# Seven products for the first q and k of an attention kernel, too, and more of V's fold beside the first scores

## The chip, the core and the metric

The kernel runs on one core of a Trainium2 chip, in one launch. The metric is the device time of an execution in microseconds (us). A core has TensorE (matrix products, with weight loads beside them), VectorE, ScalarE, GpSimd and SyncE, which here only issues DMAs. In profiles they are PE (with PEld), DVE, ACT, POOL and SP; L403 is line 403 of the kernel. Each engine works through its own instructions in order and waits for others by semaphores.

## What is computed

Four batches of 1024 tokens of width 512 go through attention, an LSTM-like gate with a causal convolution, and a feed-forward product, each followed by a layer norm. Only the attention is touched. Each of q, k, v comes from two linear layers one after the other:

```python
q = _lin(_lin(x, wq_w, wq_b), vq_w, vq_b)      # likewise k and v
q = q.reshape(b, s, hc, H).transpose(2, 0, 1, 3)   # 32 heads of 16
scores = jnp.einsum('cbqh,cbkh->cbqk', q, k) / scale
attn = jax.nn.softmax(scores, axis=-1)
o = jnp.einsum('cbqk,cbkh->cbqh', attn, v)
```

All is float32.

## The kernel before

**Folds.** The two layers of each of q, k, v are multiplied into one 512x512 matrix ("fold"), w_q, w_k (L384) and w_v (`fold_v`, L546: eight pieces of 16 matmuls, four row tiles times four column quarters, 256 columns each). The bias of the second layer plus the image of the first layer's bias is made on VectorE by `bias()` (L362 to L369). V's bias, a column, is turned into a row through DRAM: L800 writes b_d from b_vc, one element per descriptor, and L801 loads it into all partitions as b_v.

**Units, pairs and quadrants.** 32 units (batch, group of four heads). Two units make a pair p: 128 columns of w. q and k of a pair are made packed, 16 rows per head; `to_quadrants(u, which, packed)` (L398) then copies the four heads of a unit to partitions 0, 32, 64, 96 by four DMAs of 64 KB from SyncE's queue (L403). There are four such slots for q and four for k (u % 4).

**Two ways to q and k.** `project` (L407), in `qk_pieces` (L419) cut into six pieces of 176 or 160 columns, multiplies the pair's 128 columns of w by x directly: 16 matmuls per piece, with the bias added by ScalarE as it copies the result out of PSUM (L414). Only pairs 0 and 1 (units 0 to 3) are made this way. All later pairs come by twos from a scheme of Strassen's kind with seven products instead of eight (`product`, L482; `products`, L518): the 512x256 block of w and x are cut into 2x2 blocks, GpSimd makes the four sums of w's blocks (`sum_w`, L456, through `sum_blocks`, L459) and of x's (`sums_of_x`, L439; the last of the four writes over a block of x), TensorE does seven products of 8 matmuls for each 256 columns, ScalarE copies each out of PSUM (L498, L500), and GpSimd adds them together (L503 to L514). Products 2, 3 and 4 go to one of four `rooms` of 256 columns first. c11 and c12 of the result are the first pair, c21 and c22 the second.

**V.** V is made in the same way with seven products (`v_products`, L556). Of batch 0, products 1 to 3 are added by VectorE straight from PSUM (L579 to L583, with b_v, and L588); products 4 to 7 are copied to two rooms by ScalarE (L572) and added by GpSimd (L585, L588).

**Order.** It is written out by hand; in this part nothing is scheduled by a tool. A head comes first: warm-up matmuls, the folds of q and k, two pieces of `early` into PSUM tiles of `early_ps`, the rest of pair 0's q, its k, five of V's eight folds (`folds[:5]`, L794). GpSimd does the first three sums of x (L444 to L446) and pair 2's sums for q (L463 to L466) meanwhile. Then a first stage (u = -1, L851) makes only the row maxima of unit 0's scores, 32 pieces `nat` of two matmuls each (L616), whose maxima VectorE takes (L632, and L628 for those in single PSUM tiles). It goes in eleven steps, each of up to three score pieces followed by a share of `fill`: the rest of the folds, pair 1's q and k (12 pieces), the sums of V and x, 14 pieces of V, and the first six pieces of pairs 2 and 3. All pieces, and every second score piece (`apart`, two of them), take turns in the four PSUM tiles `st`; the other score pieces have two tiles of their own. After that each stage u does the exponentials of unit u and the maxima of u + 1, again with fill between.

The calls around the change:

```python
    for piece in early[2:] + qk_pieces(0, 1) + folds[:5]:        # L794
        piece()
    late_sum = sums_of_x(0)
    for work in late_sum[:3]:
        work()
    sum_w(2, 0)
    nc.sync.dma_start(b_d.rearrange("(t p) -> p t", p=P), b_vc)  # L800
    nc.sync.dma_start(b_v, b_d.partition_broadcast(P))           # L801
```

Of the kernel before, what the change touches and what calls it, by code (L numbers as in the profile page):

```python
# [8 lines left out]
F32 = mybir.dt.float32  # L9
AF = mybir.ActivationFunctionType  # L10
ALU = mybir.AluOpType
# [3 lines left out]
P = 128  # L15
B, S, D = 4, 1024, 512
# [36 lines left out]
def by_quarters(nc, pt, lhsT, rhs, tiles=FT):  # L53


    for f in range(tiles):
        for j in range(4):
            r = slice(32 * j, 32 * j + 32)
            nc.tensor.matmul(pt[r, :], lhsT(f)[:, r], rhs(f), start=f == 0, stop=f == tiles - 1)  # L59
# [193 lines left out]
def attention(ctx, tc, a, attn_d, ident, shared, hand):  # L253
# [7 lines left out]
    b_k = const.tile([P, FT], F32, tag="b_k", name="b_k")  # L261
    b_v = shared.tile([P, D], F32, tag="b_f", name="b_v")

    def big_slot(b, name):
        return shared.tile([P, NT * (D + 1)], F32, tag=f"big{b % 2}", name=name)

# [81 lines left out]
    for which, (w, v, dst) in enumerate((("wq", "vq", b_q), ("wk", "vk", b_k), ("wv", "vv", None))):  # L348
        w_n = sp.tile([P, FT, D], F32, tag="w_n", name=f"w_n{which}")
        v_t = sp.tile([P, FT, D], F32, tag="v_t", name=f"v_t{which}")  # L350
        for m in range(FT):
            rows = slice(m * P, (m + 1) * P)
            nc.sync.dma_start(w_n[:, m, :], a[f"{w}_w"][rows, :])

            (nc.scalar if which == 0 else nc.sync).dma_start(v_t[:, m, :], a[f"{v}_wT"][rows, :])
        v_n = w_v if which == 2 else rows_of_v[:, which * FT : (which + 1) * FT, :]
        w_b = sp.tile([P, D], F32, tag="w_b", name=f"w_b{which}")
        v_b = sp.tile([P, FT], F32, tag="v_bc", name=f"v_b{which}")
        if dst is None:
            dst = sp.tile([P, FT], F32, tag="b_vc", bufs=1, name="b_vc")  # L360

        def bias(w=w, v=v, dst=dst, v_n=v_n, w_b=w_b, v_b=v_b):  # L362

            nc.sync.dma_start(v_n, a[f"{v}_w"].rearrange("(t p) m -> p t m", p=P))
            nc.sync.dma_start(w_b, a[f"{w}_b"].partition_broadcast(P))
            nc.sync.dma_start(v_b, a[f"{v}_bc"])
            nc.vector.tensor_mul(v_n, v_n, w_b.unsqueeze(1).to_broadcast([P, FT, D]))
            nc.vector.tensor_reduce(dst, v_n, AX.X, ALU.add)
            nc.vector.tensor_add(dst, dst, v_b)  # L369

        if which == 2:
            bias()
            b_d = dpool.tile([D], F32, tag="b_v", bufs=1, name="b_vd")
            b_vc = dst
            break
        if which == 1:
            xts[0] = load_x(0)
        bias()
        w_d = (w_q, w_k)[which]

        pts = [ps.tile([P, D], F32, tag="ps", name=f"fold{which}_{f}") for f in range(FT)]
        for m in range(FT):
            for f in range(FT):
                nc.tensor.matmul(  # L384
                    pts[f], w_n[:, m, f * P : (f + 1) * P], v_t[:, m, :], start=m == 0, stop=m == FT - 1
                )
        for f in range(FT):
            if f % 2:
                nc.scalar.copy(w_d[:, f, :], pts[f])
            else:  # L390
                nc.vector.tensor_copy(w_d[:, f, :], pts[f])
# [6 lines left out]
    def to_quadrants(u, which, packed):  # L398
# [4 lines left out]
            nc.sync.dma_start(dst[32 * j : 32 * j + HD, :], packed[h * HD : (h + 1) * HD, :])  # L403
        if which == 0 and u >= 4:
            nc.sync.dma_start(dst[HD::32, :], dst[HD + 1 :: 32, :])

    def project(p, which, t0, n, packed, pool=None):  # L407

        b, gg = divmod(p, 4)
        w, bias = ((w_q, b_q), (w_k, b_k))[which]  # L410
        cols = slice(t0, t0 + n)
        pt = (pool or ps_st).tile([P, QW], F32, tag="ps" if pool else "st", name=f"proj{p}_{which}_{t0}")
        by_quarters(nc, pt[:, 0:n], lambda f: w[:, f, gg * P : (gg + 1) * P], lambda f: xts[b][:, f, cols])
        nc.scalar.activation(packed[:, cols], pt[:, 0:n], AF.Identity, bias=bias[:, gg : gg + 1], scale=1.0)  # L414
        if t0 + n == S:
            to_quadrants(2 * p, which, packed)
            to_quadrants(2 * p + 1, which, packed)

    def qk_pieces(p, which):  # L419

        parts = [(0, 176), (176, 176), (352, 176), (528, 176), (704, 160), (864, 160)]
        return [
            lambda pool=None, part=part: project(p, which, *part, packs[p][:, which, :], pool) for part in parts
        ]

# [28 lines left out]
    def sum_w(p, which):  # L456
        sum_blocks(blocks_of_w(p, which), [w_sums[:, which, i, :, :] for i in range(4)])
# [21 lines left out]
        rooms.append(rooms.pop(0))  # L479
        return rooms[-1]  # L480

    def product(p, which, i, t0, n):  # L482

        b, gg = divmod(p, 4)
        left, right = operands(i, blocks_of_w(p, which), [w_sums[:, which, k, :, :] for k in range(4)], b)
        cols = slice(t0, t0 + n)
        pt = ps_st.tile([P, 512], F32, tag="st", name=f"part{i}_{p}_{which}_{t0}")[:, 0:n]
        by_quarters(nc, pt, lambda k: left[:, k, :], lambda k: right[:, k, cols], 2)
        c11, c12, c21, c22 = (
            packs[which][:, o, 512 * t + t0 : 512 * t + t0 + n] for o in range(2) for t in range(2)  # L490
        )
        if i in (2, 3, 4):
            dst = room()[:, 0:n]
        else:
            dst = {1: c11, 5: c22, 6: c12, 7: c21}[i]
        if i in (1, 7):
            bias = (b_q, b_k)[which][:, gg : gg + 1] if i == 1 else b_diff[:, which, gg // 2 : gg // 2 + 1]
            nc.scalar.activation(dst, pt, AF.Identity, bias=bias, scale=1.0)  # L498
        else:
            nc.scalar.copy(dst, pt)  # L500
        add = nc.gpsimd.tensor_add
        if i == 6:
            add(c12, c12, c11)  # L503
        elif i == 2:
            add(c11, c11, dst)
        elif i == 7:
            add(c21, c21, c12)
        elif i == 5:
            add(c12, c12, c22)
            add(c22, c22, c21)  # L510
        elif i == 3:
            add(c12, c12, dst)
        elif i == 4:
            nc.gpsimd.tensor_sub(c21, c21, dst)  # L514

    due = {}

    def products(p, which):  # L518


        rows = [(2 * p - 3, 2), (2 * p - 2, 2), (2 * p - 1, 2), (2 * p, 2)]
        if which == 1:
            rows = [(2 * p - 2, 22), (2 * p - 2, 26), (2 * p - 1, 4), (2 * p, 4)]
        for n, when in enumerate(rows):
            due.setdefault(when, []).append(lambda n=n: to_quadrants(2 * p + n, which, packs[which][:, n // 2, :]))
        return [
            [
                lambda part=part: product(p, which, *part)
                for part in parts
            ]  # L530
            for parts in (
                [(1, 0, 256), (1, 256, 256), (6, 0, 256), (6, 256, 256), (2, 0, 256), (2, 256, 256)],
                [(7, 0, 512), (5, 0, 512), (3, 0, 256), (3, 256, 256), (4, 0, 256), (4, 256, 256)],
            )
        ]


    early = qk_pieces(0, 0)
    for piece in early[:2]:
        piece(early_ps)  # L540
    setup_ps.close()

    ps_st = ctx.enter_context(tc.tile_pool(name="ps_st", bufs=4, space=PSUM))
# [244 lines left out]

    folds = [lambda f=f, half=half: fold_v(f, half) for f in range(FT) for half in range(2)]

    b_diff = const.tile([P, 2, 2], F32, tag="b_diff", name="b_diff")
    for which, bias in enumerate((b_q, b_k)):
        nc.vector.tensor_tensor(b_diff[:, which, :], bias[:, 1::2], bias[:, 0::2], ALU.subtract)
    for piece in early[2:] + qk_pieces(0, 1) + folds[:5]:  # L794
        piece()
    late_sum = sums_of_x(0)
    for work in late_sum[:3]:
        work()
    sum_w(2, 0)
    nc.sync.dma_start(b_d.rearrange("(t p) -> p t", p=P), b_vc)  # L800
    nc.sync.dma_start(b_v, b_d.partition_broadcast(P))  # L801

    for u in range(-1, NU):
# [13 lines left out]
        if u == -1:  # L817
            def sums():
                sum_blocks(v_blocks, v_sums)
                late_sum[3]()  # L820

            vs = v_parts[:6] + [[(i, t), (j, t)] for t in range(4) for i, j in ((6, 7), (5, 4))]
            fill = folds[5:] + qk_pieces(1, 0) + qk_pieces(1, 1) + [sums] + [
                lambda part=part: v_products(0, part) for part in vs
            ] + fill
        elif units[u][0] + 1 < B:
            b, g = units[u][0] + 1, units[u][1]
            v1, v2 = (lambda n=n, b=b: v_products(b, v_parts[n]) for n in (2 * g, 2 * g + 1))

            fill = {  # L830
                0: fill[:2] + [v1] + fill[2:4] + [v2] + fill[4:],
                1: [v1, v2] + fill,
                2: fill[:2] + [v1] + fill[2:4] + [v2] + fill[4:],
                3: fill + [v1, v2],
            }[w]
# [439 lines left out]
```

## Time and profile before

| | us |
|---|---|
| median of 3 runs (2403.69 to 2403.97) | 2403.69 |
| the profiled execution | 2404.25 |
| its span, first to last instruction | 2402.2 |
| TensorE busy in the span | 2392.3 |
| VectorE, ScalarE, GpSimd busy | 1725.9, 1361.1, 713.0 |
| first scores (L616) start | 55.68 |
| unit 0's loop starts | 128.25 |

The page gives busy times and a chain: the work that ended last, followed back from step to step to what released it. A timeline row reads: start, length, engine, line, operation, output<-input, partitions x elements, count, and in brackets the idle time before it with what ended it. Neighbouring rows of a kind are merged, so a row's length can hold pauses. "SPq" rows are DMA issues on SyncE's queue; their length is the issue, not the transfer. A matmul in float32 is recorded twice, so 16 matmuls are "x32". Matmul ends are modelled: a busy TensorE in the stage table can still hold short waits.

### The profile page before, as it was taken

To read this page: it belongs to the slowest core of one execution; us is meant where nothing else is said; L and a number is where in the kernel's file an instruction comes from. 1 tells how busy PE (TensorE), PEld (TensorE's weight loads), DVE (VectorE), ACT (ScalarE), POOL (GpSimd) and SP (SyncE) were. 2 spreads that over 40 slices of the span, in tenths; PEclk is the share of its full clock that TensorE was granted. 3 is DMA by queue.
4 is the path that set the end of the run, shared out by engine and by line. 5 is a ranking of instruction groups with operands and counts; after the bars stand their busy time and mean duration, and the time that the engine had idled before them with its cause. 6 is when DMAs were issued, how large, how long until landed. Compare 5 with 4: busy or idle time off the path is not lost.

```text
span 2402.2 us, 70081 instructions
## 1 busy us (share of the span) xinstructions
PE 2392.3 (100%) x30124; PEld 1617.4 (67%) x30124; DVE 1725.9 (72%) x2153; ACT 1361.1 (57%) x2693; POOL 713.0 (30%) x728
## 2 busy tenths in 40 slices
PE   9999999999999999999999999999999999999998
PEld 6566666666666666666666666666666799747994
DVE  3667777777777677767677777777777477878677
ACT  1166666666666666666666666666666723411333
POOL 4332322212123322222322212211110267422761
PEclk9999999999999999999999999999999999999999
DMA  6200111011001111110111013102200242160311
GB/s 224 60 2 17 27 25 56 17 30 26 17 17 30 21 53 21 29 21 18 30 23 20 17 31 94 45 17 52 91 12 13 82 150 88 67 232 18 124 36 70
DMA packets 80838, 121.43 MB, mean 51 GB/s; under 512 B 39072, under 2 KB 39328, under 8 KB 80528
## 3 DMA queue, kind: packets, MB, share of 16 engines
q1 hardware_dynamic: 79808, 115.77, 17.0%
q8 instruction: 237, 3.88, 0.7%
q10 hardware_dynamic: 720, 1.18, 0.1%
q14 instruction: 73, 0.60, 0.1%
HBM read 80.77 MB, written 18.35 MB: 41 GB/s over the span
## 4 chain that ended last, share of the span: by engine, by line
PE 98%; DVE 0%; POOL 0%; ACT 0%; DMA 0%; issue 0%; SPq 0%; DVEq 0%; ACTq 0%; POOLq 0%
PE nat L616 22%; PE av L712 20%; PE st L686 19%; PE part L59 8%; PE pc L1017 6%; PE pa L1017 6%; PE pf L1101 4%; PE v L59 4%; PE po L59 2%; PE po L242 2%; PE proj L59 1%; PE fold L384 1%; PE tr L1093 1%; PE fold L59 1%; PE nats L616 0%; POOL v_sb L588 0%
## 5 line engine op out<-in xcount | busy, mean ns | idle before, releaser
L632 DVE TENSOR_REDUCE mx<-nat 128x2 f32<-128x1024 f32 x1008 | 1188.0, 1219 | 436.2 <-PE st L686 401.7
L697 ACT ACTIVATE at<-st 128x512 f32<-128x512 f32 x2016 | 1042.4, 603 | 477.9 <-PE st L686 467.7
L616 PE MATMUL nat<-qk 32*128 32x512 f32 x4032 | 1011.5, 614 | 0.5 <-DVE mx L632 0.5
L686 PE MATMUL st<-qk 32*128 32x256 f32 x8064 | 1001.7, 387 | 0.0
L686 PEld LDWEIGHTS st<-qk 32*128 32x128 f32 x8064 | 691.8, 184 | 43.0 <-issue 1.2
L712 PE MATMUL av<-at,v_sb 128*32 128x256 f32 x8192 | 497.7, 382 | 0.3 <-ACT at L697 0.3
L616 PEld LDWEIGHTS nat<-qk 32*128 32x128 f32 x4032 | 343.7, 184 | 220.5 <-DVE mx L632 134.6
L712 PEld LDWEIGHTS av<-at,v_sb 128*32 128x32 f32 x8192 | 241.5, 109 | 220.4 <-ACT at L697 88.4
L759 POOL TENSOR_TENSOR o_n<-o_sb,rbc 128x512 f32<-128x512 f32 x64 | 95.6, 1515 | 224.6 <-DVE mx L632 88.1
L1017 PE MATMUL pc<-xf,w 128*128 128x171 f32 x1024 | 159.7, 308 | 0.6 <-DVE o_sb L725 0.6
L1017 PE MATMUL pa<-xf,w 128*128 128x171 f32 x1024 | 159.8, 308 | 0.0
L1017 PEld LDWEIGHTS pc<-xf,w 128*128 128x128 f32 x1024 | 152.0, 189 | 1.6 <-DVE o_sb L725 1.1
L1017 PEld LDWEIGHTS pa<-xf,w 128*128 128x128 f32 x1024 | 152.0, 189 | 0.0
L1028 ACT ACTIVATE u<-u,b_c 128x512 f32<-128x512 f32 x64 | 46.2, 721 | 160.2 <-DVE u L1027 160.2
L1101 PE MATMUL pf<-w_f,xq_t 128*128 128x512 f32 (+1 forms) x264 | 114.8, 579 | 0.0
L171 POOL TENSOR_TENSOR w<-w 128x512 f32<-128x512 f32 x64 | 81.7, 1310 | 96.8 <-DMA w<-in_conv_wT 55.4
L725 DVE TENSOR_TENSOR o_sb<-av,o_sb 128x256 f32<-128x256 f32 x128 | 54.4, 425 | 68.3 <-PE av L712 67.8
L723 ACT COPY o_sb<-av 128x256 f32<-128x256 f32 x128 | 48.0, 375 | 77.8 <-PE av L712 64.5
L588 POOL TENSOR_TENSOR v_sb<-v_sb,extra 128x256 f32<-128x256 f32 x68 | 44.6, 684 | 139.8 <-ACT extra L572 139.8
L588 POOL TENSOR_TENSOR v_sb<-v_sb,rooms 128x256 f32<-128x256 f32 x56 | 36.7, 684 | 155.3 <-ACT rooms L572 155.3
L1101 PEld LDWEIGHTS pf<-w_f,xq_t 128*128 128x128 f32 x264 | 47.9, 190 | 45.8 <-issue 45.4
L1024 DVE SCALAR_TENSOR_TENSOR u<-pa,u 128x342 f32<-128x342 f32 x64 | 40.6, 634 | 50.6 <-PE pa L1017 48.0
(172 smaller groups left out, 2041.4 us busy)
## 6 DMA issues: line engine op xcount, KB each, us to landing
w<-in_conv_wT SPq DMA_DIRECT2D x32, 512.0 KB
u<-in_ctx SPq DMA_DIRECT2D x16, 1024.0 KB
xT<-in_xT SPq DMA_DIRECT2D x16, 512.0 KB
qk<-qk SPq DMA_DIRECT2D x128, 64.0 KB
qk<-extra SPq DMA_DIRECT2D x128, 64.0 KB
rbc<-rec_d SPq DMA_DIRECT2D x128, 64.0 KB
attn<-o_n SPq DMA_DIRECT2D x256, 32.0 KB
big<-attn SPq DMA_DIRECT2D x4, 2048.0 KB
```

The source lines that it names most:

```text
L59: nc.tensor.matmul(pt[r, :], lhsT(f)[:, r], rhs(f), start=f == 0, stop=f == tiles - 1)
L171: self.nc.gpsimd.tensor_tensor(w[:, i, tap, :], w[:, i, 0, :], w[:, i, 1, :], op)
L588: add(c, c, x)
L616: nc.tensor.matmul(pts[n], q_ts[u % 4][r : r + 32, qt * P : (qt + 1) * P], k_ts[u % 4][r : r + 32, kh * 512 : kh * 512 + 512], start=True, ...
L632: nc.vector.tensor_reduce(mxs[u][:, qt, 2 * pair : 2 * pair + 2, kh], pt, AX.X, ALU.max, negate=True)
L686: nc.tensor.matmul(st[:, k * QW : k * QW + QW], k_ts[u % 4][r : r + 32, kt * P : (kt + 1) * P], q_ts[u % 4][r : r + 32, qq * QW : qq * QW ...
L697: nc.scalar.activation(at, st, AF.Exp, scale=0.25)
L712: nc.tensor.matmul(av[32 * j : 32 * j + 32, :], v_sb[b % 2][:, kt, c * VW : c * VW + 32], ats[u, 2 * i + n // 2, j][:, n % 2 * QW : n % 2 ...
L725: nc.vector.tensor_add(o, av, o)
L759: nc.gpsimd.tensor_mul(o_n[:, :, half * 256 : half * 256 + 256], o_sb[:, cols].rearrange("p (s e) -> p e s", e=2), rbc[:, cols].rearrange( ...
L1017: nc.tensor.matmul(pt, w[:, i, tap, o : o + P], xf[:, tap, i, :], start=i == 0, stop=i == FT - 1)
L1101: nc.tensor.matmul(pt, xq_ts[b, t][:, f, :], hand.w_f[:, f, cols], start=f == 0, stop=f == FT - 1)
```

## The change

Pairs 0 and 1 are made by seven products together, as all other pairs: all of q and then all of k ahead of the first scores, so the first stage's fill has no `qk_pieces` any more. `project` and `qk_pieces` go. Five instead of three folds of V are left for the first stage. All four sums of x, and w's sums for q and k of pairs 0 and 1, come on GpSimd ahead of the products' adds; pair 2's sums for q follow V's sums in the first stage. The difference of biases that product 7 needs, `b_diff`, is made in `bias()`. The copies into quadrants of units 0 to 3 are all issued in the head: those of units 0 and 1 after product 3, those of 2 and 3 after product 4, for q and then for k; b_d and b_v follow them on SyncE's queue. Later instructions are the same.

```diff
+            if which < 2:
+                nc.vector.tensor_tensor(b_diff[:, which, :], dst[:, 1::2], dst[:, 0::2], ALU.subtract)
...
-    def product(p, which, i, t0, n):
+    def product(p, which, i, t0, n, pool=None):
...
-        pt = ps_st.tile([P, 512], F32, tag="st", name=f"part{i}_{p}_{which}_{t0}")[:, 0:n]
+        pt = (pool or ps_st).tile([P, 512], F32, tag="ps" if pool else "st", name=f"part{i}_{p}_{which}_{t0}")[:, 0:n]
...
+    parts_of_two = (
+        [(1, 0, 256), (1, 256, 256), (6, 0, 256), (6, 256, 256), (2, 0, 256), (2, 256, 256)],
+        [(7, 0, 512), (5, 0, 512), (3, 0, 256), (3, 256, 256), (4, 0, 256), (4, 256, 256)],
+    )
...
-    early = qk_pieces(0, 0)
-    for piece in early[:2]:
-        piece(early_ps)
+    for work in sums_of_x(0):
+        work()
+    sum_w(0, 0)
+    for t0 in (0, 256):
+        product(0, 0, 1, t0, 256, early_ps)
...
-    for which, bias in enumerate((b_q, b_k)):
-        nc.vector.tensor_tensor(b_diff[:, which, :], bias[:, 1::2], bias[:, 0::2], ALU.subtract)
-    for piece in early[2:] + qk_pieces(0, 1) + folds[:5]:
+    for which in range(2):
+        for n, part in enumerate(parts_of_two[0] + parts_of_two[1]):
+            if which == 0 and n < 2:
+                continue
+            if which == 0 and n == 2:
+                sum_w(0, 1)
+            product(0, which, *part)
+            if n in (9, 11):
+                for u in (n - 9, n - 8):
+                    to_quadrants(u, which, packs[which][:, n // 10, :])
+    for piece in folds[:3]:
         piece()
-    late_sum = sums_of_x(0)
-    for work in late_sum[:3]:
-        work()
-    sum_w(2, 0)
...
             def sums():
                 sum_blocks(v_blocks, v_sums)
-                late_sum[3]()
+                sum_w(2, 0)
...
-            fill = folds[5:] + qk_pieces(1, 0) + qk_pieces(1, 1) + [sums] + [
+            fill = folds[3:] + [sums] + [
```

More of the change, by code (lines that the diff above doesn't have):

```diff
@@ L262, in attention @@
     b_v = shared.tile([P, D], F32, tag="b_f", name="b_v")
+    b_diff = const.tile([P, 2, 2], F32, tag="b_diff", name="b_diff")
     def big_slot(b, name):
@@ L360, in attention, with bias @@
             dst = sp.tile([P, FT], F32, tag="b_vc", bufs=1, name="b_vc")
-        def bias(w=w, v=v, dst=dst, v_n=v_n, w_b=w_b, v_b=v_b):
+        def bias(w=w, v=v, dst=dst, v_n=v_n, w_b=w_b, v_b=v_b, which=which):
             nc.sync.dma_start(v_n, a[f"{v}_w"].rearrange("(t p) m -> p t m", p=P))
@@ L405, in to_quadrants @@
             nc.sync.dma_start(dst[HD::32, :], dst[HD + 1 :: 32, :])
[L407 to L424, printed above, removed]
     def blocks_of_x(b):
@@ L525, in products @@
             due.setdefault(when, []).append(lambda n=n: to_quadrants(2 * p + n, which, packs[which][:, n // 2, :]))
[L526 to L535, printed above, removed]
-    early = qk_pieces(0, 0)
-    for piece in early[:2]:
-        piece(early_ps)
+        return [[lambda part=part: product(p, which, *part) for part in parts] for parts in parts_of_two]
+    for work in sums_of_x(0):
[3 more added lines that the diff above has]
+        product(0, 0, 1, t0, 256, early_ps)
     setup_ps.close()
@@ L789, in attention @@
     folds = [lambda f=f, half=half: fold_v(f, half) for f in range(FT) for half in range(2)]
-    b_diff = const.tile([P, 2, 2], F32, tag="b_diff", name="b_diff")
-    for which, bias in enumerate((b_q, b_k)):
-        nc.vector.tensor_tensor(b_diff[:, which, :], bias[:, 1::2], bias[:, 0::2], ALU.subtract)
-    for piece in early[2:] + qk_pieces(0, 1) + folds[:5]:
+    for which in range(2):
[9 more added lines that the diff above has]
+    for piece in folds[:3]:
         piece()
-    late_sum = sums_of_x(0)
-    for work in late_sum[:3]:
-        work()
-    sum_w(2, 0)
     nc.sync.dma_start(b_d.rearrange("(t p) -> p t", p=P), b_vc)
```

## The prediction

> **What bounds the kernel now.** I read the page's busy shares and chain first, then the chain of waits from 0 to 200 us, then the SyncE queue and the stage table of the only region that the diff touches, 0 to 128 us.
>
> ```profile
> PE 2392.3 (100%) x30124; PEld 1617.4 (67%) x30124; DVE 1725.9 (72%) x2153; ACT 1361.1 (57%) x2693; POOL 713.0 (30%) x728
> ...
> PE 98%; DVE 0%; POOL 0%; ACT 0%; DMA 0%; issue 0%; SPq 0%; DVEq 0%; ACTq 0%; POOLq 0%
> ```
>
> TensorE carries 98% of the chain, so a matmul column saved is time saved, as long as nothing new makes TensorE wait. The next lines are from the chain in order of time (start, us, what): the projections and folds ahead of the first scores.
>
> ```profile
> 5.62 27.47 PE fold L384 x64
> 33.08 14.03 PE proj L59 x384
> 47.11 8.63 PE fold L59 x160
> 55.75 0.63 PE nat L616 x2
> ```
>
> Here there is no gap: five folds cover the copies of q and k into their quadrants. Those copies are DMAs of SyncE's queue, and so is V's bias, b_v (timeline, SyncE alone, two answers):
>
> ```profile
> 53.58 1.35 SPq L800 DMA_DIRECT2D b_vd<-b_vc  x1
> 63.61 0.33 SPq L801 DMA_DIRECT2D b_v<-b_vd  x1
> ```
> ```profile
> SPq L801 <- DMA b_vd<-b_vc: 8.6, 1, 8.6
> ```
>
> The row L801 matters most below: from the issue of the write of b_vd to that of the load of b_v 10.03 us pass, 8.6 of them waiting for 512 separate 4-byte elements. The load's 128 packets of 2 KB end at 69.1 us in the trace's packet records, 5.5 us after its issue. Before, this costs nothing: the first V product is added by VectorE at 90.9 us.
>
> I call 33.01 to 55.68 us the head and 55.68 to 128.25 us (where unit 0's loop begins) the first stage, 72.6 us. After 128.25 us the diff changes no instruction, so the span moves by what that point moves. The profiled execution took 2404.25 us (span 2402.2), the median of the runs is 2403.69: 0.56 lower, and I carry my difference over to it. About 0.2%, 4.8 us, is what a measurement of this kernel can tell from no change.
>
> **TensorE's own work.** A fold is 16 matmuls of 256 columns: 8.63/5 = 1.726 us. A product piece of 256 columns is 8 of the same shape, 0.863. Seven products of 512 columns make 14 pieces for q and 14 for k: 28 x 0.863 = 24.2 us, and three folds 5.2: the head grows from 22.7 to 29.3, **+6.7 us**. The first stage loses pair 1's twelve projection pieces, which the chain shows as 3.72 + 3.50 + 4.91 + 2.31 = 14.4, and gets two folds, 3.5. It also holds about 2.7 us of waits (0.65 at 63 us for VectorE, 1.3 at 116.5 to 119.7 for GpSimd's adds into v_sb through ScalarE's copies, four smaller ones); now two V pieces stand between three scores instead of three or four, GpSimd's 8 adds per two pieces take 5.5 us beside 1.91 + 2 x 1.77 = 5.45 of TensorE, so I count them gone. 72.6 - 14.4 + 3.5 - 2.7 = 59.0, **-13.6 us**. If nothing waits: -6.9 us. b_diff's two operations (0.15 us each) go from 40.6 us to before the copies of w_q and w_k; at most 0.15 us, as a fold waits there.
>
> **VectorE in the stage.** Twelve fewer pieces bring the first V products, whose four adds VectorE does itself, closer together: per step three maxima take 1.19 + 1.19 + 1.13 = 3.5 us and each V piece 4 x 0.33 = 1.33, so 6.2 us in the step with two of them against 5.45 of TensorE. Counted from the start of V's first add (0): the pieces' adds free the PSUM buffers for the scores of the fifth step at 12.3 and 13.0, where TensorE would be at 12; the stage ends at 43.6, against 42.7 of TensorE's work left there, some of it done by then. So end = start of V's first add + **43.6**. With the head at 62.4 and five folds, six scores before it (16.4 us), the first add is due at 78.8 to 79.5 (0 to 0.7 for the last k copy, which lands 2 us after its issue): end 122.4 to 123.1, a gain of 5.2 to 5.9.
>
> **The queue behind it.** This is what I think decides. Formerly pair 0's copies were issued at 40.69 and 47.60 us, b_vd after them, and pair 1's much later. Now all 32 copies stand ahead of b_vd on SyncE's queue, and the first of them wait for GpSimd's adds, not for ScalarE's copy.
>
> GpSimd: x's third sum ends at 27.45 us; the fourth, formerly at 85 us, comes now (2.36). At that point VectorE's multiply of w_b took over:
>
> ```profile
> 26.37 3.22 DVE L367 TENSOR_TENSOR rows_of_v<-rows_of_v,w_b 128x2048 f32<-128x2048 f32 x1 [5.30 <-DMA w_b<-in_wk_b]
> ...
> 27.40 2.77 POOL L463 TENSOR_TENSOR w_sums<-w_qk 128x256 f32<-128x256 f32 x1
> ```
>
> L463 takes 0.73 elsewhere: GpSimd stood 2.1 us. So the fourth sum ends near 31.9, q's four sums of w (4 x 0.73) at 34.9, k's with a second such standstill (w_v's multiply at 35.84) at 39.9. The second of q's is ready at 33.4, before product 6 at 34.7, so TensorE doesn't wait. Then eight adds to c12's last: six of 0.73, 1.27, 1.27, 1.28, that is 8.2: q's first copies at 48.1. For k, TensorE's piece ends at 55.45, and GpSimd's turn comes at 56.9: 58.3.
>
> SyncE: eight copies took 5.13, 5.9 and 6.0 us in three batches (median 0.59 each, single ones up to 1.52):
>
> ```profile
> L403 SPq DMA_DIRECT2D qk<-qk x16: 507/588/1522, 40.7 to 52.9; - x16
> ```
>
> At 0.64 each the k copies start at 58.4 and end at 68.7; at 0.70, which I take as the mean of the batches, 32 end at 70.5; at 0.80 (the slowest four later on, 3.18 us) at 73.7. Add 10.03 and 5.5: b_v lands at 84.2, **86.0** or 89.2. VectorE, in order, stands at the first V add, and behind it the maxima of the scores, and behind these TensorE for PSUM: instead of 79.5 all goes on at 86.0. End 86.0 + 43.6 = 129.6 against 128.25: **+1.4 us**, with bounds -0.5 and +4.6. The head's own delays vanish in this wait, up to 6 us. x of batch 1 is loaded 17 us later, near 90; its first use is past 128.
>
> Hidden otherwise: ScalarE's copies (0.37 to 0.58 for each 0.86 to 1.73 of TensorE), and the copies' DMA traffic. b_v's late arrival ends there, and the shift of row maxima is issued behind the load of x near 100 us, needed at 129.
>
> [...] The row: the write of b_vd is confirmed 8.6 us after its issue ends. [...] Speaking against the change: the stage table grants TensorE 1.00 in every stage, and no row has it standing for more than 2 us, so no row prices a long stop.
>
> ```profile
> 33.00:55.70 22.70, 22.70 (x549) 17.60 (x548) 5.46 (x6) 6.91 (x17) 0.00 (x0) 1.00 0.34 63
> 55.70:87.60 31.90, 31.90 (x560) 19.58 (x556) 18.67 (x24) 6.32 (x16) 7.14 (x5) 1.00 0.36 94
> 87.60:128.20 40.60, 40.34 (x602) 20.43 (x600) 27.27 (x49) 7.50 (x21) 22.21 (x36) 1.00 0.09 15
> ```
>
> (columns: length; busy us of PE, PEld, DVE, ACT, POOL; granted clock; DMA share; GB/s). [...]
>
> **Rivals.** *A, b_v comes in time*, because the write is confirmed sooner on another path of the queue or GpSimd and SyncE run less behind than I count: 5.2 to 5.9 us faster. For it: b_vd's 8.6 is a single observation. Against it: k's copies can't be issued before 56.7 (ScalarE's end and two adds after TensorE), so b_v lands before 82.5 only if the write itself is shorter by more than 3 us. *B, the queue is slower*: SyncE's copies take 0.80 or more, since 32 in a row have never been in the queue; place: b_vd's issue; price: 32 us for each us per copy, 1 us of time for 1 us of queue. It leaves 0.2% at a landing past 89.5, that is 0.81 per copy, or 0.75 with 1.6 us more elsewhere; 0.9 per copy would give +7.8. For it: single copies of 1.1 and 1.5 us. Against it: the packet records show every copy landed 2.0 to 2.2 us after its issue, far from eight in flight. *C, TensorE saves less than counted*: each product's piece costs 1.01 as it does alone between scores instead of 0.863: 28 x 0.15 = 4.1 us; but that falls into the wait too, and only the sum of A loses by it.
>
> **How the numbers follow.** Forecast (b_v bounds, within 0.2%): 0.62. A: 0.17, of which about 0.15 lies beyond 0.2%. B, with any longer pause: 0.2. C: 0.03, within 0.2%. So faster 0.15, same 0.63, slower 0.22. Time: 2403.69 + 1.4 = 2405.1. The bounds of the copies give 2403.2 to 2408.3; A reaches to 2397.8 and B to about 2412. The range leaves out part of each: 2398.5 to 2409.
>
> **What would show it.** First scores near 62.5 to 63.5 us instead of 55.7; 32 copies in one run on SyncE from 48 to 70 us; b_vd written near 70 and b_v loaded near 80; VectorE idle at its first V add for about 6 us, put down to b_v's DMA; TensorE with a hole of that length near 81 to 87; unit 0's loop at 129 to 130. Wrong if b_v's load is issued before 74 us, if VectorE's first V add follows its product at once, or if GpSimd's c12 for q is done before 46.

## The result and the profile after

The changed kernel takes **2409.18 us** (median of 11 runs, 2408.11 to 2410.82), the kernel before, run beside it, 2403.97 (11 runs, 2403.35 to 2404.9): a ratio of 1.0023, 95% interval 1.0016 to 1.0031. It is 5.2 us slower. The profiled execution took 2410.36 us, its span is 2408.4.

The busy shares and the chain's shares of the changed kernel:

```profile
PE 2393.9 (99%) x29740; PEld 1607.1 (67%) x29740; DVE 1728.0 (72%) x2153; ACT 1362.1 (57%) x2693; POOL 740.0 (31%) x758
...
PE 98%; DMA 1%; SPq 0%; DVE 0%; ACT 0%; POOL 0%; issue 0%; DVEq 0%; POOLq 0%
```

384 matmul records fewer, yet TensorE is busy 1.6 us longer, and DMA, which had no share of the chain, has 1% of it. The chain of the changed kernel in order of time (start, us, what) says where:

```profile
33.96 20.86 PE part L59 x320
...
71.39 7.49 DMA b_vd<-b_vc
78.89 6.20 DMA b_v<-b_vd
85.19 0.42 DVE v_sb L562
86.75 2.04 PE nats L599 x2
88.79 5.44 PE v L59 x64
94.22 0.63 PE nat L599 x2
```

For 14 us the end hangs on two transfers of 2 KB and 256 KB. Behind them come two rows that are too long for what they hold: two V pieces in 5.44 us (3.59 later on) and two records of a score piece in 2.04. The SyncE timeline shows the queue in front:

```profile
48.24 11.55 SPq L407 DMA_DIRECT2D qk<-qk  x16
59.90 11.37 SPq L407 DMA_DIRECT2D qk<-extra  x16
71.39 0.50 SPq L786 DMA_DIRECT2D b_vd<-b_vc  x1
78.89 0.33 SPq L787 DMA_DIRECT2D b_v<-b_vd  x1
```

The chain of waits from 64 to 134 us (engine, what, what it waited for: us in all, times, longest) shows who stood for it:

```profile
DVE v_sb L562 <- DMA b_v<-b_vd: 6.1, 1, 6.1
PE nats L599 <- DVE v_sb L566: 4.9, 1, 4.9
```

And the stage table (from:to, length, busy us of PE, PEld, DVE, ACT, POOL, granted clock, DMA share, GB/s) why the rows after it are long:

```profile
84.00:85.00 1.00, 0.00 (x0) 0.00 (x0) 0.00 (x0) 0.00 (x0) 0.92 (x2) 1.00 0.98 363
85.00:86.00 1.00, 0.00 (x0) 0.00 (x0) 0.81 (x3) 0.00 (x0) 1.00 (x3) 0.84 1.00 401
86.00:88.00 2.00, 1.25 (x2) 0.49 (x2) 2.00 (x5) 0.00 (x0) 0.48 (x1) 0.50 1.04 424
...
90.00:92.00 2.00, 2.00 (x24) 0.98 (x20) 0.13 (x1) 0.00 (x0) 0.00 (x0) 0.50 0.03 8
92.00:93.00 1.00, 1.00 (x20) 0.46 (x16) 0.57 (x2) 0.00 (x0) 0.00 (x0) 0.74 0.00 0
93.00:95.00 2.00, 2.00 (x32) 0.96 (x26) 1.54 (x6) 0.00 (x0) 0.00 (x0) 1.00 0.00 0
```

TensorE's clock is halved from about 85.7 to 92.5 us (0.84 is 0.32 of a microsecond at half; 0.74 is 0.52). It is back only when TensorE has worked again for nearly 6 us (86.75 to 92.5). Unit 0's loop starts at 133.73 us, 5.46 later than the 128.27 of before. From there on the instructions are the same; the profiled span is 6.2 longer, so nearly all of the loss is made at this point, and the other 0.7 us is not explained.

### The profile page after: what moved, and what is told of

Same layout as the page of the kernel before. It is cut to its first block, busy times and chain, and to the rows that moved or that the text cites. A ratio compares the mean times of both kernels' runs of the same rounds, so it can differ in the third digit from the quotient of the medians.

```text
span 2408.4 us, 69362 instructions
## 1 busy us (share of the span) xinstructions
PE 2393.9 (99%) x29740; PEld 1607.1 (67%) x29740; DVE 1728.0 (72%) x2153; ACT 1362.1 (57%) x2693; POOL 740.0 (31%) x758
## 3 DMA queue, kind: packets, MB, share of 16 engines
q8 instruction: 234, 3.83, 0.7%
## 4 chain that ended last, share of the span: by engine, by line
PE 98%; DMA 1%; SPq 0%; DVE 0%; ACT 0%; POOL 0%; issue 0%; DVEq 0%; POOLq 0%
PE nat L599 21%; PE av L695 20%; PE st L669 19%; PE part L59 9%; PE pc L1003 6%; PE pa L1003 6%; PE pf L1087 4%; PE v L59 4%; PE po L59 2%; PE po L242 2%; PE fold L388 1%; PE tr L1079 1%; SPq L407 0%; PE nats L599 0%; DMA b_vd<-b_vc 0%; DMA b_v<-b_vd 0%
```

## The experiments

The theory after the result: b_v comes late because its write stands behind 32 copies on SyncE's queue; VectorE (6.1 us) and then TensorE (4.9 us) stand; the stop halves the clock (0.50 until 92.5 us). The rivals: the clock costs nothing because VectorE is behind anyway (then all is b_v's lateness), and the head itself (seven products with GpSimd's adds) is the loss. Every ratio below is against the kernel before, run on the same chip. Differences from the changed kernel are between medians of separate batches, in which the kernel before read 2403.97, 2403.93, 2403.73 and 2403.70 us.

**e1: the write of b_d ahead of the products, the load of b_v between q's and k's copies.**

```diff
+    nc.sync.dma_start(b_d.rearrange("(t p) -> p t", p=P), b_vc)
     for which in range(2):
+        if which == 1:
+            nc.sync.dma_start(b_v, b_d.partition_broadcast(P))
...
-    nc.sync.dma_start(b_d.rearrange("(t p) -> p t", p=P), b_vc)
-    nc.sync.dma_start(b_v, b_d.partition_broadcast(P))
```

> The changed kernel, with b_d written ahead of all copies into quadrants and b_v loaded between q's sixteen copies and k's. Theory (the copies keep b_v back, VectorE stands 6.1 us at its first V add, TensorE 4.9 us, and TensorE's clock falls to half for some 7 us after that, 3.5 us more): the first V add follows its product near 80 us, TensorE has no hole there, the granted clock stays at 1.00 from 80 to 100 us, unit 0's loop starts near 124 instead of 133.7: 2399 to 2400 us, 4 to 5 below the kernel before. Rival 1 (the wait costs its 5.3 us, but the rest of the loss is V's pieces standing closer together beside VectorE, not the clock): about 2404. Rival 2 (the loss is made in the longer head, by the products and GpSimd's adds; b_v's wait only covers another): 2408 to 2410, with another wait in the place of b_v's.

Measured: 2403.43 us, 0.9999 (0.999 to 1.0007); 5.8 us less than the changed kernel; unit 0's loop at 127.25. No wait for b_v is left and the clock is 1.00 throughout. So the whole loss hangs on the place of these two DMAs. But the kernel now only equals the one before: the gain under it did not come, and the time is near the 2404 that the first rival gave. So far the clock is not separated from the rest; e2 does that. One part of the missing gain is a new wait. The load stands on SyncE's queue for 1.49 us ahead of k's copies, and the first scores, at 64.70, wait for one of them:

```profile
PE nat L599 <- DMA qk<-extra: 1.4, 1, 1.4
```

**e2: the changed kernel with 22 matmuls of 128 columns on idle data where TensorE stops.** They compute nothing that is used.

```diff
...
+                    if h == 11:
+                        warm = ps_nat.tile([P, 2, 512], F32, tag="nat", name="warm")
+                        for k in range(22):
+                            nc.tensor.matmul(warm[:, 0, 0:P], idle, idle, start=True, stop=True)
...
```

> The changed kernel, with 22 matmuls of zeros (128x128, some 0.22 us each, 4.8 us) into a free PSUM tile of the scores, ahead of the score piece at which TensorE stands; their result is not used. The wait for b_v is left as it is. Theory: TensorE is busy through the wait, the clock stays at 1.00, the two V pieces after it take 3.5 us instead of 5.4, the scores there 0.6 instead of 2.0: 3 to 3.5 us below the changed kernel, 2405.5 to 2406.2. Rival 1 and rival 2: no gain (2409), or up to 0.5 us lost where the matmuls end late.

Measured: 2406.67 us, 1.0012 (1.0003 to 1.002). VectorE still waits for b_v (5.4 us), but TensorE's hole is filled and the clock stays. The timeline of TensorE and VectorE, and the stage table:

```profile
80.98 5.18 PE L846 MATMUL warm<-idle 128*128 128x128 f32 x44
86.09 1.13 PE L599 MATMUL nats<-qk 32*128 32x512 f32 x4
87.15 3.66 PE L59 MATMUL v<-w_v,xT 128*32 128x256 f32 x64
```
```profile
84.00:90.00 6.00, 6.00 (x80) 4.00 (x82) 5.49 (x11) 0.00 (x0) 2.47 (x4) 1.00 0.81 326
```

Work that does nothing makes the kernel 2.5 us faster, less than the 3 to 3.5 expected. That is the clock's share of the loss, by itself; the rival of a free clock falls.

**e3: only 28 copies ahead of b_d** (unit 3's k, not needed yet, follows b_v).

```diff
-                    to_quadrants(u, which, packs[which][:, n // 10, :])
+                    if (which, u) != (1, 3):
+                        to_quadrants(u, which, packs[which][:, n // 10, :])
...
     nc.sync.dma_start(b_v, b_d.partition_broadcast(P))
+    to_quadrants(3, 1, packs[1][:, 1, :])
```

> The changed kernel, with the four k copies of unit 3 issued after b_v: 28 copies instead of 32 stand ahead of b_d. b_v lands 2.6 us earlier, near 82.5, TensorE's hole is about 2.3 us instead of 4.9. Theory: a hole of that length does not halve the clock, so 2.6 + 3.5 us are won: near 2403. Rival 1: 2.6 us, 2406.6. Rival 2: nothing, 2409.

Measured: 2404.8 us, 1.0004 (0.9995 to 1.0013), in a wide spread of 2402.63 to 2407.66. VectorE waits 2.5 us instead of 6.1, and TensorE stops for 1.34 us only. The clock falls all the same, here in the stage table of e3:

```profile
80.00:84.00 4.00, 2.66 (x12) 0.86 (x4) 2.74 (x7) 0.00 (x0) 3.94 (x4) 0.84 1.03 252
84.00:88.00 4.00, 4.00 (x34) 1.58 (x36) 2.19 (x3) 0.00 (x0) 2.09 (x3) 0.50 0.82 324
88.00:92.00 4.00, 4.00 (x46) 1.79 (x40) 2.58 (x8) 0.00 (x0) 0.00 (x0) 0.81 0.00 0
```

My belief that so short a stop is free fell with this. In the profiled run b_v is 3.25 us earlier than in e2, and unit 0's loop starts at the same time, 130.25 against 130.30: the clock took it all. Seven of e3's 11 runs list a mean clock of 0.998, four 0.999; the kernel before lists 0.999 or 1.0 in all 81 of its runs beside the experiments.

**e4: 40 copies ahead of b_d** (eight k copies issued twice).

```diff
+    for u in (2, 3):
+        to_quadrants(u, 1, packs[1][:, 1, :])
     nc.sync.dma_start(b_d.rearrange("(t p) -> p t", p=P), b_vc)
```

> The changed kernel, with the eight k copies of units 2 and 3 issued a second time (the same data to the same place), so 40 copies stand ahead of b_d. Theory: b_v lands 5.1 to 5.7 us later, near 90.5, TensorE's hole is about 10 us, the clock's fall costs again some 3.5 us: 2414 to 2415. Rival 1 the same sum. Rival 2: 2409 to 2410.

Measured: 2415.84 us, 1.0049 (1.0035 to 1.0062), four runs, 0.8 above the expected range:

```profile
DVE v_sb L562 <- DMA b_v<-b_vd: 12.1, 1, 12.1
PE nats L599 <- DVE v_sb L566: 10.9, 1, 10.9
```

Against the changed kernel's profile eight more copies put the write of b_d off by 5.24 us, 0.66 each, V's first add by 5.67 and unit 0's loop by 5.47. The queue in front of b_d is paid in full by the end. (The medians differ by 6.7, but with four runs here that spread over 2.7 us.) The clock is at half from about 84.1 to 97.8.

**e5: the kernel before, with b_d and b_v put behind pair 1's q copies.** No seven products here.

```diff
             to_quadrants(2 * p + 1, which, packed)
+            if p == 1 and which == 0:
+                nc.sync.dma_start(b_d.rearrange("(t p) -> p t", p=P), b_vc)
+                nc.sync.dma_start(b_v, b_d.partition_broadcast(P))
...
-    nc.sync.dma_start(b_d.rearrange("(t p) -> p t", p=P), b_vc)
-    nc.sync.dma_start(b_v, b_d.partition_broadcast(P))
```

> The kernel before, without the change, but with b_d's write and b_v's load put behind pair 1's eight q copies on SyncE's queue, so that b_v lands near 94.5 us, some 3.6 us after the moment (90.9) at which VectorE makes its first V add there. Theory (a late b_v costs time by itself, whatever makes q and k): VectorE stands for 3 to 4 us, 2.5 to 4 us are lost, and more if TensorE's clock falls: 2406.5 to 2408. Rival 2 (the changed kernel's loss comes from its head): within 0.5 us of the kernel before, 2404.

Measured: 2407.47 us, 1.0016 (1.0007 to 1.0025), 3.7 more than before. The profiled run is the fastest of the 11 (2406.58); its waits:

```profile
DVE v_sb L582 <- DMA b_v<-b_vd: 3.1, 1, 3.1
PE nats L619 <- DVE v_sb L586: 1.2, 1, 1.2
```

In this profile the clock stays at 1.00, after a stop nearly as long as in e3; two slower runs, at 2407.82 and 2408.97, list a mean clock of 0.998, so there it may have fallen. So a late b_v costs time without the new head, and in e1 the new head with b_v in time equals the kernel before; the rival of the head falls. From the start of its issue to the issue of the load, the write took 9.80 us here, against 10.03 before and 7.50 in the changed kernel.

**e6: e1, with b_diff made behind the copies of w_k.**

```diff
-            if which < 2:
-                nc.vector.tensor_tensor(b_diff[:, which, :], dst[:, 1::2], dst[:, 0::2], ALU.subtract)
...
+        if which == 1:
+            for n, b in enumerate((b_q, b_k)):
+                nc.vector.tensor_tensor(b_diff[:, n, :], b[:, 1::2], b[:, 0::2], ALU.subtract)
```

> e1_bv_between with the two b_diff operations moved on VectorE behind the copies of w_k. If they hold back the copies of w_q, for which a fold waits, the first product starts at 33.2 to 33.5 us instead of 33.8 and the time falls by 0.2 to 0.5 us against 2403.4; if the start of the products only varies with the first loads, nothing changes.

Measured: 2403.06 us, 1.0 (0.9991 to 1.0008). The first product starts at 33.44 instead of 33.76 us, but 0.4 us of median can't be told from nothing. Inconclusive; kept in what follows.

The profiled run, at 2405.03 us, shows something else. The first scores wait 1.75 us for a k copy (1.42 in e1), and the clock falls though nothing waits for b_v; unit 0's loop starts at 129.04, 1.8 later than in e1. From e6's stage table:

```profile
64.00:65.00 1.00, 0.17 (x1) 0.20 (x2) 0.00 (x0) 0.00 (x0) 0.00 (x0) 1.00 0.56 94
65.00:66.00 1.00, 1.00 (x6) 0.92 (x9) 0.00 (x0) 0.00 (x0) 0.00 (x0) 0.70 0.72 115
...
68.00:69.00 1.00, 1.00 (x10) 0.34 (x12) 1.00 (x3) 0.00 (x0) 0.00 (x0) 0.59 0.11 21
```

**e7: e6 with SyncE's queue in the order of need:** write of b_d, copies of units 0 and 1, b_v, copies of units 2 and 3.

```diff
-        if which == 1:
-            nc.sync.dma_start(b_v, b_d.partition_broadcast(P))
...
-                    to_quadrants(u, which, packs[which][:, n // 10, :])
+                    if u < 2:
+                        to_quadrants(u, which, packs[which][:, n // 10, :])
...
+    nc.sync.dma_start(b_v, b_d.partition_broadcast(P))
+    for which in range(2):
+        for u in (2, 3):
+            to_quadrants(u, which, packs[which][:, 1, :])
```

> e6_diff_late with another order on SyncE's queue: b_d, then the q and k copies of units 0 and 1, then b_v, then the copies of units 2 and 3. In e1 the first scores waited 1.4 us for a k copy, behind b_v and sixteen q copies. Theory: k's first copies are issued when GpSimd has made c12, near 58.5 us instead of 60.8, the first scores start at 62.3 to 63 instead of 64.7, and V's first add still doesn't wait: 1.5 to 2.5 us below e1, 2401 to 2402. If the head's length is no longer what counts (VectorE's maxima set the pace of the first stage whenever it starts): no gain, 2403.

Measured: 2401.97 us, 0.9994 (0.9984 to 1.0003). First scores at 63.42, no wait for a copy or for b_v, clock 1.00, unit 0's loop at 125.82, 2.45 earlier than before. All that I had held against the change is gone, and the gain is still not 5. The chain of e7 around the first V pieces:

```profile
76.42 1.86 PE fold L59 x32
78.29 1.73 PE v L59 x32
80.01 0.63 PE nats L600 x2
80.64 0.01 PE nat L600 x2
80.66 0.41 PE nats L600 x2
81.08 1.65 PE nats L600 x4
82.73 3.59 PE v L59 x64
```

The last group of four records of a step takes 0.84 us where nothing waits (71 and 75 us); here it takes 1.65, at 92.90 1.59. VectorE, between 80 and 98 us, has maxima and V's adds with hardly a break (17.68 of 18.00 us busy).

**e8: e7 with V's pieces in a mixed order,** so that VectorE's adds don't stand together.

```diff
+            vs = [vs[i] for i in (0, 1, 2, 6, 3, 7, 8, 4, 9, 10, 5, 11, 12, 13)]
```

> e7_order with V's pieces in a mixed order: those that VectorE adds (products 1 to 3) are no longer the first six, but alternate with those that GpSimd adds from the fourth on. In e1 TensorE waited 0.8, 0.7 and 1.0 us for VectorE's maxima. If VectorE's adds standing together are behind the first two, 1 to 1.5 us less than e7; if GpSimd's adds become late instead, no gain or up to 2 us more.

Measured: 2402.01 us, 0.9993 (0.9984 to 1.0002): the same. The waits stay where they were; that the adds stand together is not the cause of the second. The first stands behind the first V piece, which e8 leaves in its place, so e8 doesn't test it.

**e9: e7 with the pieces of products 1 and 2 on row tiles 1 and 3, and product 3, copied by ScalarE and added by GpSimd; e10: only product 3.**

```diff
-        direct = b == 0 and parts[0][0] < 4
+        direct = b == 0 and parts[0] in ((1, 0), (1, 2))
```
```diff
-        direct = b == 0 and parts[0][0] < 4
+        direct = b == 0 and parts[0][0] < 3
```

> The kernel of e7 (biases' difference later; write of V's bias row ahead of the products; SyncE's order: units 0 and 1, load of b_v, units 2 and 3) with four of V's six first pieces (products 1 and 2 of row tiles 1 and 3, both pieces of product 3) copied out by ScalarE and added by GpSimd instead of VectorE. Theory (what keeps the stage above the 59.0 us of my sum is VectorE alone: three maxima and V's adds per step, which hold PSUM back): VectorE loses 8 adds on row tiles 1 and 3 and 4 of product 3, 12 x 0.33 = 4.0 us; GpSimd stands idle from 86 to 98 and has room for them; TensorE's waits for VectorE at 81 and 93 us (1.65 and 1.59) go, unit 0's loop starts at 122.6 to 124 instead of 125.8, time 2399 to 2400.5. Rival (GpSimd's adds, 0.65 us each against 0.33, come late and hold the two pairs of rooms, so the wait is only moved to ScalarE's copies): 125.5 to 127, time 2402 to 2403.

> The kernel of e7 with only product 3 of V (two pieces, four adds in all) copied out by ScalarE and added by GpSimd. Theory (VectorE's load): 4 x 0.33 = 1.3 us less on VectorE, past the first of its two waits; the second wait (1.59 at 93 us) goes, the first (1.65 at 81 us) stays: unit 0's loop at 124.3 to 125, time 2400.5 to 2401.3. Rival (rooms and GpSimd take it back): 125.8 or later, 2402 or more.

Measured: e9 2401.21 us, 0.999 (0.9981 to 0.9999); e10 2401.68, 0.9992 (0.9983 to 1.0001). Unit 0's loop starts at 125.27 and 125.56, against 125.82. Both missed the theory's numbers. I had read 1.65 and 1.59 as waits, but each group holds 0.84 us of work: the waits are 0.81 and 0.75. The second shrinks in both, the first stays, as the chain of e9 shows:

```profile
80.92 1.65 PE nats L600 x4
...
92.74 1.20 PE nats L600 x4
```

VectorE's load does cost time, but only what its waits hold. The rival's numbers (from 125.5 and 2402 in e9, from 125.8 and 2402 in e10) were not met either: both runs lie between, and no wait for GpSimd's adds is seen in e9. e9 is the fastest median of all; e7, e9 and e10 overlap and can't be ranked, and only e9's interval stays below 1.

## Why the prediction was wrong

The forecast was 2405.1 us, within 0.2% of before, the range 2398.5 to 2409.0. The time is 2409.18: 4.1 above the forecast, 0.2 above the range, and slower by a little over 0.2%.

- **The queue: right, in part by luck.** SyncE's copies start at 48.24 (48.1 foretold), k's at 59.90 (58.4), b_d is written at 71.39 (70.5), b_v lands at 85.14 (86.0). One copy costs 0.72 (0.70). That b_v's landing is only 0.9 off is luck: the write was issued 0.9 later than counted and its load landed 0.75 later after its issue, but the write took 7.50 us instead of 10.03. VectorE stands 6.1 us (about 6). GpSimd's two standstills are there: its fourth sum of x takes 4.41 us (2.36 + 2.1 foretold), its row of w 2.78. (The prediction counts eight adds to c12's last and six scores ahead of V's first add; its 8.2 and 16.4 us are those of nine adds and nine scores, and 8.15 and, in e7, 16.7 were measured.)
- **The head: short by 1.0.** The 28 pieces take 24.2 us (24.2), the first scores come at 63.34 (62.5 to 63.5). But the first product starts at 33.89, 0.9 later than the first projection did. Moving b_diff gave 0.3 of this (e6 against e1), twice the 0.15 I had allowed, but the runs scatter: five profiles without the move start at 33.45 to 33.89, five with it at 32.80 to 33.44. The rest is open. In the changed kernel it vanished in the wait for b_v.
- **"VectorE in the stage", end = start of V's first add + 43.6: failed.** Measured from V's first add to unit 0's loop: e7 80.08 to 125.82, 45.74; e2 84.51 to 130.30, 45.79; the changed kernel 85.19 to 133.73, **48.54**; e3 81.26 to 130.25, 48.99. So the term was 2.1 to 2.2 too small where the clock stays, and 4.9 to 5.4 where it falls.
- **"No row prices a long stop", so the sum had nothing for the clock: the larger half of the miss.** 48.54 - 45.79 = 2.75 us in the profiles, 2.5 in the medians (e2).

With these the miss adds up: b_v 0.8 earlier than counted, the term 2.2 longer, the clock 2.75: 129.6 - 0.8 + 2.2 + 2.75 = 133.75, measured 133.73.

Why the term was 2.2 short, and the stage longer than its 59.0: by e7's rows TensorE's work there is 20.5 for the scores (32 x 1.92/3), 9.0 for five folds, 25.0 for 14 V pieces, 5.45 for six product pieces, 60.0 in all. By the same prices the stage of before held 60.0 + 14.4 - 3.6 = 70.8 of work, so 1.8 us of waits and not 2.7. I took 0.9 us of work for waits. And e7's stage is 62.4 long, 2.4 more than this work: 0.81 and 0.75 are the two waits for VectorE, and the last step's two score pieces take 2.10 us in the chain (121.05 to 123.15), where the 60.0 counts 1.28; two of their weight loads are put down to VectorE's maxima. From V's first add on, the same prices give 43.4 of work where the prediction had 42.7, and these waits are 2.4 where it had 0.9 (43.6 against 42.7): 0.7 and 1.5 are the 2.2. It had foreseen a wait 12.3 to 13.0 us after the first add (e7's second comes at 12.8), not those at 1 us and in the last step.

The rivals: A (b_v in time, 5.2 to 5.9 us faster) had too high a price; with b_v in time by construction the medians of e7 and e9 are 1.8 and 2.5 us lower than before, and only e9's interval stays below 1. B, the queue slower, is not what happened; the cost came after the queue. C was not seen: the pieces took 0.86.

**The clock.** The stage tables show the clock at half for 6.84 us in the changed kernel, 6.84 in e3 (82.68 to 89.52 by windows of 1 us), 13.66 in e4 and 3.42 in e6 (65.40 to 68.82): twice, twice, four times and once the same length. Why, no run shows. Nor does one length of a stop bring the fall: in the changed kernel it comes 3.83 us into a stop of 4.90, in e4 2.56 us into one of 10.86, in e3 1.21 us into one of 1.34, and in e6 0.57 us after one of 1.75 has ended. In the 3.4 us before these falls, about as long as e6's clock is at half, TensorE worked for 0, 0.85, 2.20 and 1.66 us.

The length of the work does not sort them by itself: 3.4 us that hold all of e1's stop of 1.42 us hold 2.0 us of work, less than e3's 2.20, and e1's clock stayed. But 1.9 of e3's 2.20 us were score pieces, which use 32 of 128 rows, while e1's stop comes behind fold pieces on all 128. Whether that makes the difference, no run tried.

## What to carry to other kernels

When a change makes a queue longer, look for the small old DMA behind it that had slack, and price not only the wait but TensorE's clock after it: here 32 copies of 0.72 us brought 6.1 us of wait, and the clock 2.5 us more. Keep a queue in the order of need (e7, which but for b_diff only reorders, took back 7.2 us), and if TensorE must stop, try idle matmuls in the hole: here they were 2.5 us cheaper than a halved clock (e2). Before a gap in a sum is called a wait, take its own work off it: a group of 1.65 us held 0.84 of work, and 0.9 of the stage's "waits" were work.

## What was not expected of the hardware

- A stop of TensorE of 1.34 us, among short matmuls on 32 rows, came with a clock at half for 6.8 us (e3), one of 1.75 us with 3.4 us of it (e6); stops of 1.42 us in e1 and 1.22 us in e5 left it at 1.00 in the profiled runs. Runs of e3 and of e6 spread over 5.0 us, those of e1 over 2.5.
- The runs of the changed kernel lie in two groups, 2408.1 to 2409.2 and 2410.1 to 2410.8. Three of the five upper runs list a mean clock of 0.997, all six lower ones 0.998, so a longer fall may be part of it; but the profiled run, an upper one, lists 0.998.
- A DMA of 512 elements of 4 bytes, DRAM its target, was confirmed 7.50, 9.33, 9.80 and 10.03 us after the start of its issue, in the changed kernel, e4, e5 and the kernel before, which do the same write.
